# Four chained layers on one core: layer 0's early loads in one queue, the bias table split in compact form and reversed by ScalarE, and batch-norm scales spread from rows

## The chip, the cores and the metric

The kernel runs on one core of one Trainium2 chip. The core has five engines with instruction streams of their own: TensorE (PE, with its weight loads PEld), VectorE (DVE), ScalarE (ACT), GpSimd (POOL) and SyncE (SP). SP, ACT and POOL issue DMAs, which 16 DMA engines carry out. The metric is the device time of one execution in microseconds; the kernel before took 2920.96 us (median of three executions, 2919.23 to 2924.84).

## The reference

The input `x` has the shape (T, B, N, D) = (4, 8, 512, 512), float32. Four layers follow each other, each of the form x + f(groupnorm(x)), with groups of two of the 8 channels (B):

```python
x = x + _L0_conv_ref(_gn(x), ...)   # spiking attention
x = x + _L1_conv_ref(_gn(x), w)     # 13x13 Gaussian, per channel
x = x + _L2_conv_ref(_gn(x), ...)   # 3x3, quantised, 8 channels
x = x + _L3_conv_ref(_gn(x), ...)   # 3x3, 8 channels
```

The change is in layer 0, cut to what matters here (`lif` is a leaky spiking neuron stepping through T; H = 8 heads of 64):

```python
def bn(x, g, b, m, v):
    return g * (x - m) * jax.lax.rsqrt(v + EPS) + b
q = heads(lif(bn(x @ Wq.T, ...)))          # k and v likewise
scores = jnp.einsum('tbhnd,tbhmd->tbhnm', q, k) * scale
rel = pos[None, :] - pos[:, None] + (N - 1)
bias = bias_table[rel].transpose(2, 0, 1)   # table: (1023, 8)
out = jnp.einsum('tbhnm,tbhmd->tbhnd', scores + bias[None, None], v)
out = lif(out) * gate_scale + gate_shift
out = lif(bn(out @ Wp.T, ...))
```

Scores have no softmax, so q (k v) is computed instead of (q k) v. The bias is a Toeplitz matrix for each head: element (n, m) is the table's entry m - n + 511.

## The kernel before

**Order of the work.** The program is written in Python; a scheduler fixes the order of the instructions on each engine when the program is built, and each engine then runs its list strictly in order, waiting on semaphores for others. `tc.issue_after(op)` puts the instructions of a block behind `op` in the lists of engines. Of DMAs that SP and ACT issue, eight are under way at most: each uses one of eight semaphores, and the next on the same one waits for it. Tiles come from pools; tiles with one tag share its buffers, and a new tile waits until the last use of the one before it in that buffer.

**Layer 0** goes through 32 steps (b, t), one image of 512 x 512 each. A step needs the group statistics (mean, deviation) of channel pair g = b // 2 at time t, so two images per group and t; the one that is worked on comes as `xq` (`load_quarters`, four DMAs with rows of 512 B), the other only for its statistics as `xs` (`load_x`, four tiles). The statistics of step 0 are eight `bn_stats` (L431) and a chain of small instructions between VectorE, TensorE (`gps`, L181) and GpSimd (L178 to L198). `transpose` (L618, L480) normalises the image and transposes it in four pieces `xn`. `project_in` (L499) multiplies by the weights `w_v`, `w_k` and `w_q` (the latter two halves of one tile `w_kq`), in four column blocks c of four matmuls each; each 128x512 float32 matmul leaves two records in the trace. VectorE turns each block into spikes. `attend` then multiplies: `ps_kv` (L515), `ps_a` (L527, q times kv) and `ps_b` (L535, the bias times v); `fire` makes the spikes `so`, and `project_out` (L562) multiplies these by `wp` and adds the residual. The next step's projections are interleaved with `project_out` of the present one.

**Preparations in the first step.**

- `batch_norms` turns the 72 columns of `cols` into a scale and an offset for each feature: `a_half`, `c_half`. For q these are used as columns. For v, k and p the scale is multiplied into the weights (L349) and the offset is a tile `c_twice`, so both are wanted along the free dimension, the same in all partitions. `along_free` (L330 to L340) makes that: VectorE scales the identity by one column (`diag`, L336), TensorE multiplies it by ones (L337), four times for 512 features.
- `load_weights`: `w_v` goes out on SP ahead of `xs`; `w_k` and `w_q` go out on ACT's queue behind ScalarE's instruction that writes `c_v` (L350).
- `prepare_bias` (L353 to L369): a Toeplitz row block of a head needs, in partition p, the table's entries from p on, reversed. So each of 8 heads is loaded as a Hankel matrix of 128 x 896 float32 (`hankel`, each partition's row one entry further), and split in three bfloat16 parts `toep` that add up to the float32 value. ScalarE copies the reversed rows to the first part (L365), VectorE subtracts (L366), ScalarE copies the rest (L367), GpSimd subtracts (L368), ScalarE copies again (L369). Two heads are under way at once.
- `prepare_out` loads W_p (1 MB) on ACT's queue, makes p's offset with 16 small matmuls (`shift`, L382), and splits the scaled W_p in two parts `wp` on VectorE and ScalarE (L401 to L407).
- `bands1` builds layer 1's band matrices. Its scratch tile `bands` has the tag `h_p`, which the bias table's second tile `rest` has too. It clears the taps' rows on VectorE (L729), loads the taps (L731), and TensorE's `ps_band` (L741) waits for these; it stands in TensorE's list ahead of the larger part of step 0's attention.

**Layers 1 to 3** are not touched. Layer 1 reads layer 0's result from DRAM through band matmuls (L815), layers 2 and 3 run together (L1118, L1221).

The functions that the diff touches, with the line numbers of the profile:

Of the kernel before, what the change touches and what calls it, by code (L numbers as in the profile page):

```python
# [129 lines left out]
def network(ctx: ExitStack, tc: tile.TileContext, i: dict, out: bass.AP):  # L130
# [30 lines left out]
    nc.vector.tensor_scalar_mul(avg_same, same, 1.0 / n_half)  # L161
# [65 lines left out]
    with ExitStack() as s:  # L227
        head = layer0(
            s, tc, i, x_in, x1d, ident, block, avg, group_stats, st1, norm1, band1d, r1, w_sum, shared
        )  # L230

# [35 lines left out]
def layer0(  # L267
# [43 lines left out]
    ones = wpool.tile([P, P], F32, name="ones")  # L311
    nc.vector.memset(ones, 1.0)

    def batch_norms():

        neg_half = wpool.tile([P, 4, NC], F32, name="nh0")
        nc.vector.memset(neg_half, -0.5)
        nc.vector.tensor_scalar_add(a_half, bn[:, :, 3, :], EPS)
        nc.gpsimd.tensor_tensor(a_half, a_half, neg_half, op=ALU.pow)
        nc.vector.tensor_mul(a_half, a_half, bn[:, :, 0, :])  # L320
        nc.vector.tensor_scalar_mul(a_half, a_half, 0.5)
        c = c_half[:, :3, :]
# [3 lines left out]
        nc.vector.scalar_tensor_tensor(  # L326
            c, bn[:, :3, 1, :], 0.5, c, op0=ALU.mult, op1=ALU.add
        )
# [16 lines left out]
    def prepare_in(n):  # L345
        j = "qkvp".index(n)
        scale = along_free(a_half[:, j, :])
        for k in range(NC):
            nc.vector.tensor_mul(wT[n][:, k, :], wT[n][:, k, :], scale)  # L349
        return nc.scalar.mul(c_twice[n], along_free(c_half[:, j, :]), 2.0).ins  # L350

    def prepare_bias():


        n_u = toep[0].shape[2]
        table = i["table"]
        hankel = state.tile([P, 2, n_u], F32, tag="h_o", name="hankel")
        rest = state.tile([P, 2, n_u], F32, tag="h_p", name="rest")
        for h in range(H):
            src, r = hankel[:, h % 2, :], rest[:, h % 2, :]  # L360
            nc.scalar.dma_start(
                src, bass.AP(table.tensor, h * (2 * N - 1), [[1, P], [1, n_u]])
            )
            dst = [w[:, h, :] for w in toep]
            nc.scalar.copy(dst[0], src[:, ::-1])  # L365
# [3 lines left out]
            nc.scalar.copy(dst[2], r)  # L369
# [6 lines left out]
    def prepare_out(wp32):  # L376
# [3 lines left out]
        for e in range(NC):  # L380
# [11 lines left out]
        nc.vector.scalar_tensor_tensor(c, bn[:, 3, 1, :], 0.5, c, op0=ALU.mult, op1=ALU.add)  # L392

        nc.scalar.mul(
            c_twice["p"].rearrange("p (g v) -> p g v", g=PH), phases(along_free(c)), 2.0
        )
        scale = work.tile([P, D], F32, tag="v", name="scale_p", bufs=3)
        nc.scalar.copy(scale, along_free(a_half[:, 3, :]))
# [256 lines left out]
    for n in range(-1, last + 1):  # L655
# [39 lines left out]
        if n < 0:  # L695
            with ExitStack() as behind:
                for op in first:
                    behind.enter_context(tc.issue_after(op))
                prepare_bias()
# [620 lines left out]
```

## Time and profile before

| what | us |
|---|---|
| median of three executions | 2920.96 (2919.23 to 2924.84) |
| profiled execution: own time | 2921.53 |
| profiled execution: span, first to last instruction | 2919.3 |
| TensorE busy in the span | 2819.7 (97%) |
| VectorE busy | 2208.5 (76%) |
| GpSimd busy | 888.1 (30%) |
| ScalarE busy | 551.0 (19%) |
| DMA, mean over the span | 110 GB/s, 322.10 MB |

The span leaves out what lies before the first and after the last instruction, 2.2 us here. In timelines each line has the start and the duration in us, the engine (ACTq and SPq are issues of DMAs), the line of the code, the operation, the tiles written and read, and in brackets how long the engine had been idle and what ended that wait. Lines of the same kind that follow each other are merged: "x8" and the time of all of them. The granted clock is the share of full speed that TensorE's clock was given in a stretch.

### The profile page before, as it was taken

To read this page: it belongs to the slowest core of one execution; us is meant where nothing else is said; L and a number is where in the kernel's file an instruction comes from. 1 tells how busy PE (TensorE), PEld (TensorE's weight loads), DVE (VectorE), ACT (ScalarE), POOL (GpSimd) and SP (SyncE) were. 2 spreads that over 40 slices of the span, in tenths; PEclk is the share of its full clock that TensorE was granted. 3 is DMA by queue.
4 is the path that set the end of the run, shared out by engine and by line. 5 is a ranking of instruction groups with operands and counts; after the bars stand their busy time and mean duration, and the time that the engine had idled before them with its cause. 6 is when DMAs were issued, how large, how long until landed. Compare 5 with 4: busy or idle time off the path is not lost. (4 is left out here: it accounts for less than half of the span.)

```text
span 2919.3 us, 36593 instructions
## 1 busy us (share of the span) xinstructions
PE 2819.7 (97%) x12865; PEld 1301.8 (45%) x12865; DVE 2208.5 (76%) x3916; ACT 551.0 (19%) x860; POOL 888.1 (30%) x1928
## 2 busy tenths in 40 slices
PE   6899999999999999999999999999999999679999
PEld 3454455554555554455455555545333333223334
DVE  7898688688779868877886886796665566888870
ACT  1300010010010001001000100110111121677774
POOL 3243233334224333323432343332311111232220
PEclk9899999999999999999999999999999999999999
DMA  7332322222322222222222111112877778699975
GB/s 180 96 81 78 79 62 63 70 70 77 73 59 66 69 75 74 69 59 67 69 70 59 45 52 52 52 52 62 226 202 207 201 212 220 170 199 238 219 193 147
DMA packets 323895, 322.10 MB, mean 110 GB/s; under 512 B 21431, under 2 KB 237183, under 8 KB 323599
## 3 DMA queue, kind: packets, MB, share of 16 engines
q1 hardware_dynamic: 261872, 237.39, 33.4%
q0 software_dynamic: 19776, 56.14, 6.0%
q10 hardware_dynamic: 42063, 26.23, 3.2%
q8 instruction: 101, 1.65, 0.3%
q14 instruction: 83, 0.68, 0.1%
HBM read 210.57 MB, written 103.60 MB: 108 GB/s over the span
## 5 line engine op out<-in xcount | busy, mean ns | idle before, releaser
L499 PE MATMUL ps_in<-w_v,xn 128*128 128x512 f32 x1024 | 459.5, 599 | 3.0 <-DVE xn L480 3.0
L499 PE MATMUL ps_in<-w_kq,xn 128*128 128x512 f32 x1024 | 450.1, 592 | 0.0
L815 PE MATMUL ps_conv<-x,bt 112*64 112x512 f32 x2048 | 445.2, 592 | 0.8 <-DVE v_p L467 0.8
L499 PE MATMUL ps_in<-xn,w_kq 128*128 128x512 f32 x1024 | 444.6, 592 | 0.0
L535 PE MATMUL ps_b<-toep,vtok 128*64 128x512 bf16 x3072 | 368.2, 383 | 1.0 <-DVE v_o L550 1.0
L450 ACT ACTIVATE h_q<-v_q,c_half 128x512 f32<-128x512 f32 x96 | 69.2, 721 | 1473.1 <-DVE v_q L446 852.3
L475 POOL TENSOR_TENSOR h_v<-h_v,c_v 128x512 f32<-128x512 f32 x96 | 121.9, 1270 | 686.0 <-DVE h_v L474 660.0
L584 POOL COPY x1s<-x1s 128x2 f32<-128x2 f32 (+1 forms) x1024 | 227.7, 277 | 273.3 <-DVE x1s L573 273.3
L562 PE MATMUL ps_out<-wp,so 128*128 128x512 f32 x1024 | 308.9, 444 | 0.0
L499 PEld LDWEIGHTS ps_in<-xn,w_kq 128*128 128x128 f32 x1024 | 194.3, 190 | 233.0 <-issue 222.0
L499 PEld LDWEIGHTS ps_in<-w_kq,xn 128*128 128x128 f32 x1024 | 194.2, 190 | 219.9 <-issue 205.0
L499 PEld LDWEIGHTS ps_in<-w_v,xn 128*128 128x128 f32 x1024 | 191.0, 191 | 218.5 <-issue 210.2
L815 PEld LDWEIGHTS ps_conv<-x,bt 112*64 112x64 f32 x2048 | 146.4, 135 | 288.9 <-issue 286.5
L535 PEld LDWEIGHTS <-vtok 128*64 128x64 bf16 x3072 | 175.6, 111 | 154.7 <-issue 5.6
L1221 PE MATMUL ps_conv<-x,band_t 64*64 64x512 f32 x2040 | 242.6, 595 | 0.0
L562 PEld LDWEIGHTS ps_out<-wp,so 128*128 128x128 f32 x1024 | 192.6, 188 | 94.4 <-issue 57.8
L1125 DVE SCALAR_TENSOR_TENSOR x<-ps_conv,inv,x 128x512 f32<-128x512 f32 (+1 forms) x172 | 187.4, 1185 | 45.7 <-PE ps_conv L1118 45.6
L573 DVE SCALAR_TENSOR_TENSOR x1s<-v_p,xr 128x256 f32<-128x256 f32 x256 | 188.5, 776 | 14.9 <-DMA x<-x1s 4.1
L837 POOL DMA_DIRECT2D x<-xo x128 | 71.6, 566 | 330.8 <-ACT xo L822 316.4
L822 ACT ACTIVATE xo<-ps_conv,off 128x512 f32<-128x512 f32 x128 | 87.8, 688 | 431.1 <-PE ps_conv L815 310.2
L475 POOL TENSOR_TENSOR h_k<-h_k,c_k 128x512 f32<-128x512 f32 x96 | 123.2, 1284 | 134.0 <-DVE h_k L474 134.0
L1118 PE MATMUL ps_conv<-xq,band 128*128 128x512 bf16 (+1 forms) x516 | 132.2, 393 | 30.3 <-POOL xq L1101 30.3
(193 smaller groups left out, 3161.4 us busy)
## 6 DMA issues: line engine op xcount, KB each, us to landing
x<-x SPq DMA_DIRECT2D x64, 917.0 KB
x<-x SPq DMA_DIRECT2D x168, 256.0 KB
x<-x1s POOLq DMA_DIRECT2D x128, 262.0 KB, 2.6
xq<-in_x SPq DMA_DIRECT2D x128, 256.0 KB
xr<-in_x SPq DMA_DIRECT2D x128, 256.0 KB
out<-o SPq DMA_DIRECT2D x164, 192.0 KB
xs<-in_x SPq DMA_DIRECT2D x112, 256.0 KB
x<-xo ACTq DMA_DIRECT2D x128, 128.0 KB
```

The costliest lines, as they stand in the source:

```text
L475: nc.gpsimd.tensor_add(h, h, c_twice[n])
L499: mm = nc.tensor.matmul(ps, lhsT=lhsT, rhs=rhs, start=k == 0, stop=k == NC - 1)
L535: nc.tensor.matmul(pb[two * DH : (two + 1) * DH, :], lhsT=v[:, c, h * DH : (h + 1) * DH], rhs=toep[z][:, h, u : u + N], start=c == 0 and z ...
L562: nc.tensor.matmul(ps, lhsT=so[:, k, c * P : (c + 1) * P], rhs=wpT[z][:, k, :], start=k == 0 and z == 0, stop=k == NC - 1 and z == 1,)
L573: nc.vector.scalar_tensor_tensor(own, v.rearrange("p (g v) -> p g v", g=PH)[:, two, :], 1.0, by_phase[:, two, :], op0=ALU.is_ge, op1=ALU.add,)
L584: nc.gpsimd.tensor_copy(x1[:, f, u : u + n], x1[:, fm, um - n + 1 : um + 1][:, ::-1])
L815: mm = nc.tensor.matmul(ps[q * M1 : (q + 1) * M1, :], lhsT=bt[:, z, :], rhs=xt[:, w0 : w0 + N_PS1, z : z + NV], start=z == 0, stop=z == SH ...
L822: nc.scalar.activation(xo[:, a, :], ps, AF.Identity, bias=off[:, t : t + 1])
L837: engine.dma_start(bass.AP(dst.tensor, dst.offset + (q * n_half * W1_OUT * B + b) * D + f * NV, [[B * D, W1_OUT], [W1_OUT * B * D, n_half] ...
L1118: mm = nc.tensor.matmul(ps[:n_p, :], lhsT=w["band2"][:n_p, j, dx, :n_p], rhs=xq[:, j, dx : dx + PH, :], start=dx == 0, stop=dx == 2,)
L1125: done["DVE"] = nc.vector.scalar_tensor_tensor(own.rearrange("p (v g) -> p g v", g=PH), by_phase(ps[:n_p, :]), w["inv"][:n_p], by_phase(x[ ...
L1221: mm = nc.tensor.matmul(ps[j][b * HALF : (b + 1) * HALF, :], lhsT=band[half, b, dx, :], rhs=x3[half, s0 + j, dx : dx + D], start=dx == 0, ...
```

## The change

It has four parts.

1. **Loads.** Step 0's `xq`, then `xs`, then the weights of v, k and q all go out on SP in this order. The weights of k and q no longer wait for `c_v`. The batch norms are built first, and the loads' consumers come behind them in VectorE's list. `avg_same`, which waits for the constants' DMA, is now written behind layer 0 in the code.
2. **Scales from rows.** `as_rows_of` transposes all scale columns at once (16 rows of 128) and all offsets at once (12 rows), and copies them from PSUM to SBUF on ScalarE. `along_free` then needs four matmuls whose stationary operand is one column of the identity, broadcast over 128 columns: it picks one row and spreads it over the partitions. The `diag` products on VectorE and the tile `ones` go. For p, the scale comes before the offset now.
3. **The bias table's split.** The table (8 x 1023) is loaded once as 24 x 341, split in its three bfloat16 parts there (five VectorE instructions on 24 partitions), and the parts are written to DRAM as 3 x 8184.
4. **The bias table's turn.** For each pair of heads and each part, a Hankel tile of 128 x 2 x 896 bfloat16 is loaded from these, and one ScalarE copy writes it reversed to `toep`. That is 12 loads and 12 copies. The tile takes the buffer `h_o` if h + z is odd (z = 1) and `h_p` if it is even (z = 0 and z = 2).

In the built program, VectorE's scalings of `w_v` stand behind step 0's transposes, ScalarE's first Hankel loads stand behind its copy of `c_k`, and the statistics sums (`gps`) of steps 1 and 2 come later in TensorE's list than before. W_p's load stands between the first two Hankel loads and the third.

```diff
-    nc.vector.tensor_scalar_mul(avg_same, same, 1.0 / n_half)
...
+    nc.vector.tensor_scalar_mul(avg_same, same, 1.0 / n_half)
...
-    ones = wpool.tile([P, P], F32, name="ones")
-    nc.vector.memset(ones, 1.0)
...
-    def along_free(cols):
+    def as_rows_of(cols):
+
+        n = cols.shape[1]
+        ps = ps_mm.tile([n, P], F32, tag="mm", name="ps_rows")
+        nc.tensor.transpose(ps, cols, ident)
+        rows = wpool.tile([4 * NC, P], F32, tag="rows", name="rows", bufs=2)
+        nc.scalar.copy(rows[:n], ps)
+        return rows[:n]
+
+    def along_free(rows, j):
 
 
+        n = rows.shape[0]
         ps = ps_mm.tile([P, D], F32, tag="mm", name="ps_free")
         for c in range(NC):
-            diag = work.tile([P, P], F32, tag="diag", name="diag", bufs=2)
-            nc.vector.tensor_scalar_mul(diag, ident, cols[:, c : c + 1])
+            at = NC * j + c
             nc.tensor.matmul(
-                ps[:, c * P : (c + 1) * P], lhsT=ones, rhs=diag, start=True, stop=True
+                ps[:, c * P : (c + 1) * P], lhsT=ident[:n, at : at + 1].to_broadcast([n, P]),
+                rhs=rows, start=True, stop=True,
             )
         return ps
...
     def prepare_in(n):
         j = "qkvp".index(n)
-        scale = along_free(a_half[:, j, :])
+        scale = along_free(a_rows, j)
         for k in range(NC):
             nc.vector.tensor_mul(wT[n][:, k, :], wT[n][:, k, :], scale)
-        return nc.scalar.mul(c_twice[n], along_free(c_half[:, j, :]), 2.0).ins
-
-    def prepare_bias():
-
-
-        n_u = toep[0].shape[2]
-        table = i["table"]
-        hankel = state.tile([P, 2, n_u], F32, tag="h_o", name="hankel")
-        rest = state.tile([P, 2, n_u], F32, tag="h_p", name="rest")
-        for h in range(H):
-            src, r = hankel[:, h % 2, :], rest[:, h % 2, :]
-            nc.scalar.dma_start(
-                src, bass.AP(table.tensor, h * (2 * N - 1), [[1, P], [1, n_u]])
-            )
-            dst = [w[:, h, :] for w in toep]
-            nc.scalar.copy(dst[0], src[:, ::-1])
-            nc.vector.tensor_sub(r, src[:, ::-1], dst[0])
-            nc.scalar.copy(dst[1], r)
-            nc.gpsimd.tensor_sub(r, r, dst[1])
-            nc.scalar.copy(dst[2], r)
+        return nc.scalar.mul(c_twice[n], along_free(c_rows, j), 2.0).ins
+
+    n_h, n_u = 2 * N - 1, toep[0].shape[2]
+
+    def split_bias():
+
+        n_e = n_h // 3
+        parts = tc.dram_tile([3, H * n_h], BF16, name="bias_parts")
+        src = state.tile([3 * H, n_e], F32, tag="h_o", name="bias_table")
+        nc.scalar.dma_start(src, bass.AP(i["table"].tensor, 0, [[n_e, 3 * H], [1, n_e]]))
+        part = state.tile([3 * H, 3, n_e], BF16, tag="h_p", name="bias_part")
+        for z in range(3):
+            nc.vector.tensor_copy(part[:, z, :], src)
+            if z < 2:
+                nc.vector.tensor_sub(src, src, part[:, z, :])
+        nc.scalar.dma_start(
+            bass.AP(parts.tensor, parts.offset, [[n_e, 3 * H], [H * n_h, 3], [1, n_e]]), part
+        )
+        return parts
+
+    def prepare_bias(parts):
+
+
+        for h in range(0, H, 2):
+            for z in range(3):
+                hankel = state.tile(
+                    [P, 2, n_u], BF16, tag="h_o" if (h + z) % 2 else "h_p", name="hankel"
+                )
+                nc.scalar.dma_start(
+                    hankel,
+                    bass.AP(
+                        parts.tensor, parts.offset + (z * H + h) * n_h, [[1, P], [n_h, 2], [1, n_u]]
+                    ),
+                )
+                nc.scalar.copy(toep[z][:, h : h + 2, :], hankel[:, :, ::-1])
...
-    load(0)
-    load_weights("v", nc.sync)
-    statistics(0, 0, 0, as_rows(xs[0]))
-    statistics(0, 0, 1, load_x(1, 0, "xs"))
-    batch_norms()
+    normed = batch_norms()
+    a_rows = as_rows_of(a_half.rearrange("p n c -> p (n c)"))
+    c_rows = as_rows_of(c_half[:, :3, :].rearrange("p n c -> p (n c)"))
+    with tc.issue_after(normed):
+        load(0)
+        statistics(0, 0, 0, as_rows(xs[0]))
+        statistics(0, 0, 1, load_x(1, 0, "xs"))
+        for n in "vkq":
+            load_weights(n, nc.sync)
+        bias_parts = split_bias()
     for k in range(NC):
         transpose(0, k)
-    with tc.issue_after(prepare_in("v")):
-        load_weights("k", nc.scalar)
-        load_weights("q", nc.scalar)
+    prepare_in("v")
```

Left out of the diff: in `prepare_out`, p's scale is spread and copied ahead of p's offset (which goes through `as_rows_of`), and the call of `prepare_bias` passes the parts.

More of the change, by code (lines that the diff above doesn't have):

```diff
@@ L325, in batch_norms @@
         )
[L326 removed]
+        op = nc.vector.scalar_tensor_tensor(
             c, bn[:, :3, 1, :], 0.5, c, op0=ALU.mult, op1=ALU.add
         )
[L330 removed]
+        return op.ins
+    def as_rows_of(cols):
[7 more added lines that the diff above has]
+        n = rows.shape[0]
         ps = ps_mm.tile([P, D], F32, tag="mm", name="ps_free")
         for c in range(NC):
[L335 to L336 removed]
+            at = NC * j + c
             nc.tensor.matmul(
[L338 removed]
+                ps[:, c * P : (c + 1) * P], lhsT=ident[:n, at : at + 1].to_broadcast([n, P]),
+                rhs=rows, start=True, stop=True,
             )
@@ L392, in prepare_out @@
         nc.vector.scalar_tensor_tensor(c, bn[:, 3, 1, :], 0.5, c, op0=ALU.mult, op1=ALU.add)
+        scale = work.tile([P, D], F32, tag="v", name="scale_p", bufs=3)
+        nc.scalar.copy(scale, along_free(a_rows, 3))
         nc.scalar.mul(
-            c_twice["p"].rearrange("p (g v) -> p g v", g=PH), phases(along_free(c)), 2.0
+            c_twice["p"].rearrange("p (g v) -> p g v", g=PH), phases(along_free(as_rows_of(c), 0)), 2.0
         )
-        scale = work.tile([P, D], F32, tag="v", name="scale_p", bufs=3)
-        nc.scalar.copy(scale, along_free(a_half[:, 3, :]))
         for k in range(NC):
@@ L698, in layer0 @@
                     behind.enter_context(tc.issue_after(op))
-                prepare_bias()
+                prepare_bias(bias_parts)
                 prepare_out(load_out())
```

## The prediction

> **What bounds the kernel now.** First the page's busy shares and slices:
>
> ```profile
> PE 2819.7 (97%) x12865; PEld 1301.8 (45%) x12865; DVE 2208.5 (76%) x3916; ACT 551.0 (19%) x860; POOL 888.1 (30%) x1928
> PE   6899999999999999999999999999999999679999
> ```
>
> TensorE is busy 97% of the span. The holes are the first two slices (146 us) and one near 2,500 us, where layer 1 gives way to layer 2. The diff touches layer 0's start only, and of the built programs' orders of instructions TensorE's agree again some 380 instructions in, the others' within the first two steps. A gain in the first slices moves everything behind it forward, since TensorE idles only 1.9 us between 200 and 250 us. So I read the head in stretches of 20 us (busy time of each engine, TensorE's granted clock, DMA share, GB/s):
>
> ```profile
> 0.00:20.00 20.00, 4.74 (x16) 3.71 (x16) 8.35 (x28) 1.88 (x2) 4.42 (x8) 1.00 0.97 191
> 20.00:40.00 20.00, 8.97 (x24) 5.09 (x25) 11.41 (x26) 0.00 (x0) 1.92 (x2) 1.00 0.89 213
> 80.00:100.00 20.00, 16.68 (x104) 9.92 (x104) 17.18 (x27) 10.59 (x13) 7.16 (x4) 0.74 0.63 144
> 100.00:120.00 20.00, 9.60 (x44) 5.13 (x45) 14.79 (x32) 7.87 (x13) 0.38 (x1) 0.58 0.41 116
> 120.00:140.00 20.00, 20.00 (x77) 9.29 (x74) 16.77 (x34) 3.06 (x5) 7.35 (x14) 1.00 0.09 29
> ```
>
> There are two holes: before about 40 us, with the DMA engines full, and 80 to 120 us, with TensorE often idle and at a low clock. From 120 us it is full. The timeline tells what ends the first:
>
> ```profile
> 22.43 1.36 DVE L431 BATCH_NORM_STATS2 st<-xs 128x6 f32<-128x512 f32 x2 [5.26 <-DMA xs<-in_x]
> 25.48 0.17 DVE L178 TENSOR_REDUCE gsum_x<-st 128x1 f32<-128x16 f32 x1
> 30.96 5.60 PE L499 MATMUL ps_in<-w_v,xn 128*128 128x512 f32 x8 [3.00 <-DVE xn L480]
> ```
>
> The first projection starts at 30.96, 5.5 us after the last statistics, which waited for `xs`. In the second hole TensorE's own timeline reads:
>
> ```profile
> 79.44 3.93 PE L382 MATMUL shift<-cols,wp 128*128 128x1 f32 x32
> 107.90 1.91 PE L741 MATMUL ps_band<-bands 13*52 13x128 f32 x8 [6.76 <-DMA bands<-in_w]
> 112.50 0.56 PE L181 MATMUL gps_x<-gsum_x,avg 128*128 128x1 f32 x2 [2.68 <-DVE gsum_x L178]
> 131.76 2.43 PE L562 MATMUL ps_out<-wp,so 128*128 128x512 f32 x8
> ```
>
> Its three projections end at 79.4; `ps_band` waits until 107.9; the first output projection, my mark for "the head is over", comes at 131.8. `bands` lies in the buffer `h_p`, which the bias table frees last:
>
> ```profile
> 69.24 0.33 ACTq L361 DMA_DIRECT2D hankel<-in_table  x1
> 70.66 2.10 DVE L504 TENSOR_SCALAR k<-v_k 128x512 bf16<-128x512 f32 x1
> 72.51 0.94 ACT L369 CAST toep<-rest 128x896 bf16<-128x896 f32 x1 [2.40 <-DMA hankel<-in_table]
> 86.32 0.34 ACTq L361 DMA_DIRECT2D hankel<-in_table  x1
> 94.11 0.94 ACT L365 CAST toep<-hankel 128x896 bf16<-128x896 f32 x1 [1.31 <-DMA hankel<-in_table]
> 101.17 0.94 ACT L369 CAST toep<-rest 128x896 bf16<-128x896 f32 x1
> ```
>
> The last piece is copied at 102.1; from there to `ps_band` are 5.8 us (memset, the taps' DMA). A head's rows took 3.3 us from issue (69.24) to use (72.51) with nothing else moving, 7.8 us (86.32 to 94.11) beside the loads of step 2.
>
> **What the Trainium skill says.** "DMA: Bandwidth & Descriptors", section "Issuing engines are not separate DMA queues": DMAs of all issuers run on the same 16 engines and interleave. The trace agrees: `xs` went out with w_k and w_q from the other queue at a DMA share of about 1.05, and came late. "ScalarE: Activation LUTs", section "What ACT_TABLE_LOAD costs": with immediate operands 186 ns plus 0.833 ns an element, fp32 and bf16 alike. That gives 932 ns for 896 elements; the trace has 936, reversed reads included, and 618 for 512. "GPSIMD Engine Reference", section "1. Specifications": its SBUF interfaces are shared with VectorE. The trace agrees: the threshold above took 2.10 us while GpSimd subtracted (70.19 to 72.48), about 0.4 otherwise. "TensorE: Matmul & The Clock Gate", part 1: half clock after an idle window, until it has been busy about 3.4 us; the trace shows 0.50 granted from 104 to 120 us.
>
> **The change, part by part.**
>
> *Loads in order.* Ahead of the first normalisation must land xq and xs (1.05 MB each), c128 (0.18), cols and the table (0.07): 2.35 MB. In the trace 2.1 MB had moved by 12 us at some 215 GB/s, so `xs` is complete at 13, not 24. One statistics instruction (0.7) and the 5.5 us chain make 19.2; but the scalings of w_v, formerly done while waiting, now stand behind the transposes: three further transposes (1.85) and the first scaling (0.67) give 21.7 for the first projection, 9.2 earlier. w_v lands by 18.1 (another 1.05 MB), w_k by 23, w_q by 28, ahead of need at about 21, 35 and 51. Ahead of it all VectorE gets five passes over 24x341 elements (2 us by 128x512 rows of 0.4 to 0.7) that wait for the table's 33 KB: cols, first in that queue, landed at 3.85, xq needs 7, so they cost nothing. If the table came 10 us late, the statistics behind it would be as late.
>
> *Scales from rows.* VectorE loses 24 `diag` instructions of 0.28 us, and TensorE its waits for them. The first four matmuls (5.4, from 30.96) end at 27.1; eight small ones at 0.3 end at 29.5; 44 matmuls at 0.87 (two records of 0.434: 32 in 13.90) end at 67.8, some 68 with two statistics sums. Before: 79.4. That is 11.4 earlier.
>
> *Bias table.* Off the engines go 8 VectorE subtractions (1.08), 8 GpSimd ones (1.9) with the stretching they cause, and 24 ScalarE copies (22.5 us); 12 ScalarE copies of 1792 elements come (estimate by the skill's price 1.68; 20.2 us), and 12 loads of 459 KB in rows of 1792 B for 8 in rows of 3584 B. There are two buffers, and z = 0 and z = 2 share one, so eight loads and copies go one after the other through `h_p`; the order pairs the first four with one in `h_o`. The first goes out behind the c_k copy, at 29.5. For a load I take 3.7 alone (3.3 plus 0.4 for shorter rows, a guess), 5.5 beside others, 1.7 for a pair's second. Round 1, beside xq and xs of step 1: 29.5 + 5.5 + 1.7 + 1.7 = 38.4. Round 2 stands behind the 1.05 MB of w_p: 1.97 MB at half of 300 GB/s end at about 43, lands 46 and 47.7, copied 49.4. Rounds 3 and 4: 7.1 each, 63.6. Two singles at 5.5: 74.6; two beside step 2's loads at 7.3: 89.2. Plus the same 5.8: `ps_band` at 95, 12.9 earlier. Bounds of a load: 3.3 and 7.8 us, both measured. ScalarE's h_q copies and w_p casts stand between the later copies, with VectorE's results behind them; those inputs come at 57 to 80 us, and I count nothing.
>
> *After `ps_band`.* Before: 23.9 us to the mark. The 2.7 us wait for a statistics sum goes (it now stands behind the projection), about 1 us of waits for v_o too: 20.2, hence 115.2. That is 16.6 earlier; I take 16. Moving `avg_same` is nothing: its reader is in layer 2.
>
> Against the profiled execution (2921.53 around a span of 2919.3; 0.6 above the median 2920.96) this gives 2905.5, against the median **2905.0**.
>
> **Rivals.**
>
> *The bias chain is hidden.* With 3.3 us for every load and no delay by w_p the chain is 29.5 + 4 x 6.7 + 4 x 5.0 = 76, `ps_band` 82, the mark 102; TensorE's own work from 68 (w_p sums 3.9, attention 14, eight matmuls 7, small ones 2) allows 95. That is 2891 at 102, 2884 at the floor. Against it: w_p and step 1's loads are in the same engines.
>
> *The serial chain becomes the bound (slower).* If each load takes the loaded 7.8 us, four paired rounds of 11.2, w_p's 5 and four singles of 9.5 end at 117, `ps_band` at 123, the mark at 143: 11 later, 2932. For it: one buffer for eight transfers, 5.5 MB instead of 3.7, half the row length. Against it: from 64 to 70 us the DMA engines were empty. It decides from a chain end of about 106, 2 us more on each of eight rounds.
>
> *Only the start is gained, or nothing.* If the chain ends near 100, the mark is at 126: 2915. If it also stalls w_p's casts, nothing is left: 2921. A bf16 copy at twice the estimated price would do it (20 us).
>
> **How the numbers follow.** What a measurement of this kernel tells from no change is about 0.2%, 5.8 us. Main case (2898 to 2912) 0.55; hidden chain 0.15; start only, 2912 to 2915, 0.11; within 0.2% 0.10; slower 0.09. Faster is 0.81. Leaving out about one in ten below and above gives 2890 to 2922.
>
> **What would show it.** First projection near 21.7 us, projections done near 68, last bias copy near 89, `ps_band` near 95, the mark near 115; TensorE idle from about 78 to 95, and GpSimd without subtractions. An early first projection with a mark beyond 126 means the load chain was mis-sized; a first projection at 28 or later, that the single queue is slower than 215 GB/s or the table's load held VectorE. A shift at the mark unlike that of the end would refute that TensorE carries it on.

## The result and the profile after

The changed kernel takes 2902.18 us (median of four executions, 2901.55 to 2903.70) against 2920.60 for the kernel before in the same measurement (2919.23 to 2924.84). The ratio is 0.9936, 95% interval 0.9924 to 0.9948: faster by 0.64%, or 18.4 us. The profiled execution took 2902.63 us around a span of 2900.8, against 2921.53 and 2919.3 before: the span is 18.5 us shorter, and what lies around it is the same to 0.4 us.

Line numbers shift with the diff: the projections are now L524, `ps_band` L769, the mark's `ps_out` L587, the reversing copies L394 and the Hankel loads L388.

First the page's busy shares and TensorE's slices:

```profile
PE 2818.8 (97%) x12868; PEld 1302.5 (45%) x12868; DVE 2183.1 (75%) x3888; ACT 549.2 (19%) x851; POOL 868.8 (30%) x1920
PE   7999999999999999999999999999999999689999
```

TensorE has the same work as before (2818.8 against 2819.7 us). VectorE has 25 us less and GpSimd 19 us less, and neither difference is the gain: the gain is idle time of TensorE, by far the most of it in the first two slices (some 2 us lie between 1150 and 1480 us, see the last part on the prediction). The stretches show it (length, busy time of PE, PEld, DVE, ACT and POOL, granted clock, DMA share, GB/s):

```profile
0.00:20.00 20.00, 5.64 (x22) 4.66 (x22) 11.16 (x32) 2.39 (x4) 4.95 (x9) 1.00 0.85 192
20.00:40.00 20.00, 17.34 (x46) 8.43 (x47) 11.84 (x21) 3.97 (x3) 2.53 (x2) 1.00 0.78 184
80.00:100.00 20.00, 13.69 (x90) 7.40 (x88) 11.86 (x23) 8.53 (x15) 0.00 (x0) 0.70 0.64 154
100.00:120.00 20.00, 19.75 (x83) 9.61 (x79) 19.33 (x43) 3.05 (x6) 5.73 (x13) 1.00 0.48 125
120.00:140.00 20.00, 19.70 (x56) 10.18 (x55) 19.11 (x34) 0.00 (x0) 13.67 (x26) 1.00 0.22 77
```

From 20 to 40 us TensorE is busy for 17.3 us where it was 9.0, and from 100 to 120 us for 19.75 where it was 9.6. The second hole is down to one stretch, 80 to 100 us. GpSimd's subtractions are gone there (7.16 us of work before, none now).

The timeline, TensorE's but for the first line:

```profile
14.83 0.17 DVE L177 TENSOR_REDUCE gsum_x<-st 128x1 f32<-128x16 f32 x1
22.66 5.94 PE L524 MATMUL ps_in<-w_v,xn 128*128 128x512 f32 x8 [5.35 <-DVE w_v L359]
...
70.80 6.30 PE L407 MATMUL shift<-cols,wp 128*128 128x1 f32 x32
89.68 0.64 PE L552 MATMUL ps_a<-q,kvb 128*64 128x512 f16 x2 [2.33 <-DVE kvb L545]
93.87 1.91 PE L769 MATMUL ps_band<-bands 13*52 13x128 f32 x8 [3.56 <-DMA bands<-in_w]
111.25 2.11 PE L587 MATMUL ps_out<-wp,so 128*128 128x512 f32 x8
...
222.48 0.64 PE L552 MATMUL ps_a<-q,kvb 128*64 128x512 f16 x2 [2.89 <-DVE kvb L545]
```

The statistics are summed at 14.83 instead of 25.48, the first projection starts at 22.66 instead of 30.96, `ps_band` at 93.87 instead of 107.90, the mark comes at 111.25 instead of 131.76. Between the projections' end (68.9) and 87.3 us TensorE has no gap. It is slow there, though: the 16 one-column matmuls of `shift` (32 records) take 6.30 us where they took 3.93, and in finer stretches the granted clock is 0.50 from 71.6 to 81.8 us.

ScalarE's timeline has the bias table's loads (ACTq) and copies:

```profile
30.68 0.92 ACTq L388 DMA_DIRECT2D hankel<-bias_parts  x2
...
46.37 3.27 ACT L394 COPY toep<-hankel 128x1792 bf16<-128x1792 bf16 x2 [7.74 <-DMA hankel<-bias_parts]
...
77.73 1.69 ACT L394 COPY toep<-hankel 128x1792 bf16<-128x1792 bf16 x1 [2.06 <-DMA hankel<-bias_parts]
79.45 0.37 ACTq L388 DMA_DIRECT2D hankel<-bias_parts  x1
...
85.88 0.25 ACT L336 COPY rows<-ps_rows 4x128 f32<-4x128 f32 x1 [5.34 <-PE ps_rows L334]
...
87.09 1.68 ACT L394 COPY toep<-hankel 128x1792 bf16<-128x1792 bf16 x1
```

The bias chain, from the issue of the first load to the end of the last copy, runs from 30.68 to 88.77, which is 58.1 us; before, it was 57.6 (44.49 to 102.11). It is no shorter, it starts earlier. In this execution its last link is not a load: ScalarE stood for 5.34 us at the copy of the rows of p's offset, which waits for TensorE, and the last bias copy is behind that in ScalarE's list.

### The profile page after: what moved, and what is told of

Read it like the earlier page. It is cut to its first block, busy times and chain, and to the rows that moved or that the text cites. A ratio compares the mean times of both kernels' runs of the same rounds, so it can differ in the third digit from the quotient of the medians.

```text
span 2900.8 us, 36559 instructions
## 1 busy us (share of the span) xinstructions
PE 2818.8 (97%) x12868; PEld 1302.5 (45%) x12868; DVE 2183.1 (75%) x3888; ACT 549.2 (19%) x851; POOL 868.8 (30%) x1920
## 5 line engine op out<-in xcount | busy, mean ns | idle before, releaser
L524 PE MATMUL ps_in<-w_v,xn 128*128 128x512 f32 x1024 | 459.1, 599 | 5.4 <-DVE w_v L359 5.4
L524 PE MATMUL ps_in<-w_kq,xn 128*128 128x512 f32 x1024 | 449.8, 592 | 0.0
L524 PE MATMUL ps_in<-xn,w_kq 128*128 128x512 f32 x1024 | 444.9, 592 | 0.0
L587 PE MATMUL ps_out<-wp,so 128*128 128x512 f32 x1024 | 308.7, 444 | 0.0
L524 PEld LDWEIGHTS ps_in<-xn,w_kq 128*128 128x128 f32 x1024 | 194.3, 190 | 232.5 <-issue 220.4
L524 PEld LDWEIGHTS ps_in<-w_kq,xn 128*128 128x128 f32 x1024 | 194.3, 190 | 220.7 <-issue 206.2
L524 PEld LDWEIGHTS ps_in<-w_v,xn 128*128 128x128 f32 x1024 | 191.4, 191 | 222.9 <-issue 212.1
L587 PEld LDWEIGHTS ps_out<-wp,so 128*128 128x128 f32 x1024 | 192.6, 188 | 94.0 <-issue 57.8
```

The lines of the kernel that those rows point to most:

```text
L524: mm = nc.tensor.matmul(ps, lhsT=lhsT, rhs=rhs, start=k == 0, stop=k == NC - 1)
L587: nc.tensor.matmul(ps, lhsT=so[:, k, c * P : (c + 1) * P], rhs=wpT[z][:, k, :], start=k == 0 and z == 0, stop=k == NC - 1 and z == 1,)
```

## The experiments

All kernels compute the whole result. "Median" is the time of a kernel; the ratio is that to the kernel before, run on the same chip.

### What each of three parts carries

Each kernel is the changed one with one part put back.

**The old making of the bias table**, with the new loads and rows kept:

```diff
-        bias_parts = split_bias()
...
-                prepare_bias(bias_parts)
+                prepare_bias()
```

Here `prepare_bias` is the old one: 8 float32 Hankel loads, 24 copies, subtractions on VectorE and GpSimd.

> The changed kernel with the bias table made the old way (8 float32 Hankel loads, three ScalarE copies, one VectorE and one GpSimd subtraction a head); loads and scales stay changed. Theory A, the bias rework carries part of the gain (it frees VectorE and GpSimd and shortens the chain): last bias copy after 92 us, ps_band after 97, time 2906 to 2912. Theory B, the gain comes from the earlier start alone, since the chain from the first Hankel load to the last copy was 57.6 us before (44.5 to 102.1) and is 58.1 now (30.7 to 88.8): the old chain, started some 14 us earlier, ends by 88, first projection at 20.5 because the split is gone from the front of VectorE's list, time 2898 to 2903.

Measured: 2911.22 (2910.08 to 2913.58), ratio 0.9971 (0.9959 to 0.9983). The first projection starts at 22.14, 0.5 us earlier without the split on 24 partitions. The last bias copy ends near 92.8, `ps_band` comes at 101.92, the mark at 121.33. The chain is 63.1 us long here (29.70 to 92.77), 5 more than in the changed kernel. Part of what is lost is no bias chain at all. A line of TensorE's timeline of this kernel, and two that lie side by side on GpSimd and VectorE:

```profile
73.46 0.59 PE L180 MATMUL gps_x<-gsum_x,avg 128*128 128x1 f32 x2 [7.56 <-DVE gsum_x L177]
...
42.66 2.06 POOL L378 TENSOR_TENSOR rest<-rest,toep 128x896 f32<-128x896 f32 x1
42.90 2.37 DVE L484 SCALAR_TENSOR_TENSOR h_v<-v_v 128x512 f32<-128x512 f32 x1
```

VectorE is busy for 18.5 of the 20 us from 40 to 60 us, against 10.7 in the changed kernel, and so is late with the next step's statistics. Only 3.3 us of that are its own subtractions. Four other instructions of that stretch take 2.1 to 2.4 us instead of 0.4 to 0.7, each of them while GpSimd subtracts. So the old subtractions cost VectorE more through GpSimd than by its own share.

**The old order of loads:**

```diff
+    load(0)
+    load_weights("v", nc.sync)
+    statistics(0, 0, 0, as_rows(xs[0]))
+    statistics(0, 0, 1, load_x(1, 0, "xs"))
+    batch_norms()
...
-        for n in "vkq":
-            load_weights(n, nc.sync)
...
+    with tc.issue_after(prepare_in("v")):
+        load_weights("k", nc.scalar)
+        load_weights("q", nc.scalar)
```

> The changed kernel with the loads as before: w_v on SP ahead of xs, w_k and w_q on ACT's queue behind c_v, statistics ahead of the batch norms in the code. Theory A and B: first projection at 30 to 32 us, the first Hankel load at 38 to 40, everything behind it 8 us later, time 2909 to 2912. Rival, the start is covered by later waits (the wait for ps_band and the cold clock): first projection as late, but the mark (first output projection) within 4 us of 111, time 2903 to 2906.

Measured: 2910.11 (2909.42 to 2910.60), ratio 0.9966 (0.9953 to 0.9979). The first projection starts at 33.04, the first Hankel load is issued at 40.32, the last bias copy ends at 95.7, `ps_band` comes at 99.76 and the mark at 119.38. A start that is 10.4 us later makes the end 7.9 us later. The start is also later than was expected, and 2.1 us later than in the kernel before: VectorE's wait for `xs` ends at 25.17 here, at 22.43 there. So this variant costs a little more than the old order did in its own kernel.

**The old `diag` products** in place of the rows:

```diff
-            at = NC * j + c
+            diag = work.tile([P, P], F32, tag="diag", name="diag", bufs=2)
+            nc.vector.tensor_scalar_mul(diag, ident, cols[:, c : c + 1])
             nc.tensor.matmul(
-                ps[:, c * P : (c + 1) * P], lhsT=ident[:n, at : at + 1].to_broadcast([n, P]),
-                rhs=rows, start=True, stop=True,
+                ps[:, c * P : (c + 1) * P], lhsT=ones, rhs=diag, start=True, stop=True
             )
```

> The changed kernel with scales and offsets spread by the old diag products (24 VectorE instructions) instead of rows. If the rows pay, as the prediction had it (TensorE's waits for diag between the first blocks, 2.2 us of the 11.4 by the end of the projections): first projection within 1 us of 22.7, projections done at 70.5 to 73, time 2904 to 2907. Rival, VectorE has room at that time (busy 54% from 40 to 60 us) and hides them: within 1 us of 2902.

Measured: 2910.32 (2907.65 to 2911.56), ratio 0.9963 (0.9949 to 0.9977): a miss, by some 3 us to the slow side. First projection 25.57 (expected within 1 us of 22.7), projections done at 72.4, first Hankel load 36.28, `ps_band` 99.06, mark 117.88. From VectorE's and ScalarE's timelines:

```profile
12.86 2.46 DVE L449 BATCH_NORM_STATS2 st<-xq 128x6 f32<-128x512 f32 x4
36.21 0.60 ACT L353 ACTIVATE c_k<-ps_free 128x512 f32<-128x512 f32 x1 [22.96 <-PE ps_free L340]
```

The rows do more than take work from VectorE: without them ScalarE's copy of `c_k` comes 5.6 us later (36.21 instead of 30.61), and the whole bias chain hangs on that copy. Of these, 2.9 us are there at the start: the first `diag` products stand ahead of the statistics in VectorE's list, which begin at 12.86 instead of 9.94. In the kernel before they cost nothing there, as the last statistics waited for `xs` until 22.43. And only 4.3 of the 8.1 us arise in the head: step 3's first `ps_kv` starts at 287.80 instead of 283.47. The rest comes between 1150 and 1480 us, as is told in the part on the prediction.

Putting one part back costs 9.0, 7.9 and 8.1 us; that is 25.0 for three parts of a change that gains 18.4. The costs are not to be added up: each of the parts delays the start of the same bias chain, or lengthens it, and the variants have costs that the kernel before did not have (the start of the old loads, `diag` ahead of the statistics).

### Is the length of the bias chain what sets the end?

**Longer: all Hankel tiles in one buffer.**

```diff
-                    [P, 2, n_u], BF16, tag="h_o" if (h + z) % 2 else "h_p", name="hankel"
+                    [P, 2, n_u], BF16, tag="h_p", name="hankel"
```

> The changed kernel with all twelve Hankel tiles in the buffer h_p, so loads and copies go strictly one after the other: the rival mechanism of the prediction, made worse on purpose. If the end of the chain decides, as I hold: 12 rounds of about 5.9 us (4.2 load, 1.7 copy) and some 4 for w_p from 30.7 give a last copy near 105, ps_band near 111, the mark near 127, time 2916 to 2921. Rival, TensorE is held by something else (the copy of c_p's rows and the product kvb, not the table): ps_band within 5 us of 93.9, time within 5 us of 2902.

Measured: 2915.83 (2912.67 to 2918.62), ratio 0.9984 (0.9978 to 0.9991); the time is just below what was expected, and so is the mark; the last copy (105.4) is where it was expected. TensorE's timeline:

```profile
97.52 0.64 PE L552 MATMUL ps_a<-q,kvb 128*64 128x512 f16 x2 [8.09 <-ACT v_o L570]
...
105.43 2.35 PE L560 MATMUL ps_b<-toep,vtok 128*64 128x512 bf16 x20 [1.30 <-ACT toep L394]
108.81 1.04 PE L769 MATMUL ps_band<-bands 13*52 13x128 f32 x8 [1.02 <-DMA bands<-in_w]
```

Now TensorE waits longest for `v_o` (8.09 us), which stands behind a bias copy in ScalarE's list, and then for `toep` itself (1.30). A chain end 16.6 us later makes the mark 12.7 us later (123.97) and the end 13.7 by the medians (11.4 between the profiled executions): a longer chain costs most of its length.

**Shorter: strict alternation of the two buffers**, so that two loads in a row never use the same one. It was run twice on one chip, the second time together with the changed kernel:

```diff
-                    [P, 2, n_u], BF16, tag="h_o" if (h + z) % 2 else "h_p", name="hankel"
+                    [P, 2, n_u], BF16, tag="h_o" if (3 * h // 2 + z) % 2 else "h_p", name="hankel"
```

> The changed kernel with the twelve Hankel tiles in strict alternation over h_o and h_p, so that one loads while the other is copied. If the end of the chain alone decides: last bias copy near 77 us instead of 88.8, ps_band near 83, the mark (first output projection) near 100, time 2891 to 2895. If, with the chain out of the way, ps_band falls to the next thing in line (the taps' load stands behind W_p's casts in ACT's list, and these behind the copy of c_p's rows, which waits for TensorE): last copy near 77, but ps_band at 91 to 95, time within 4 of 2902.

> Strict alternation of the buffers once more: 2900 within 1.5 us, and 1 to 3 us below the changed kernel on the same chip.

> The changed kernel once more, with nothing edited, on the same chip as the two others: 2902 within 1.5 us; the mark at 111.3 within 0.5 us. If it lies more than 2 us from 2902.2, differences of 2 us between kernels are not told apart by runs on different chips.

Measured: alternation 2900.09 (2899.07 to 2901.33), ratio 0.9931 (0.9916 to 0.9946), the second time 2903.89 (2902.03 to 2904.97), ratio 0.9942 (0.9930 to 0.9955); the changed kernel again 2903.58 (2902.09 to 2905.36), ratio 0.9942 (0.9929 to 0.9954). The last copy ends at 77.5 and 79.4, 11 and 9 us earlier than in the changed kernel's profile above (9 and 7 earlier than in its second one, where it ends at 86.2), and the time is the same. What looked like 2 us in the first measurement did not come back in the second. The alternation's own two measurements differ by 3.8 us, on one chip, so differences of up to 4 us between measurements are not read from here on.

Where the 9 us go is seen in the second run of the alternation, in VectorE's timeline and one line of TensorE's:

```profile
79.94 1.16 DVE L426 SCALAR_TENSOR_TENSOR wp_k<-wp,cols,scale_p 128x512 f32<-128x512 f32 x1 [5.37 <-ACT scale_p L419]
...
88.79 0.61 DVE L545 TENSOR_TENSOR kvb<-ps_kv,c 128x512 f16<-128x512 f32 x1
89.46 0.64 PE L552 MATMUL ps_a<-q,kvb 128*64 128x512 f16 x2 [5.23 <-DVE kvb L545]
```

ScalarE's copy of `scale_p` stands behind the last two bias copies. VectorE waits 5.37 us for it, then does the whole preparation of W_p, and `kvb` is behind that in its list. The TensorE wait that was for the bands in the kernel before (6.76 us) is now for the larger part one for `kvb` (5.23; 2.75 for the bands are left), and VectorE starts `kvb` no earlier than in the changed kernel (88.79 against 88.94, and 86.13 in that kernel's second profile).

**The rows of p's offset copied by VectorE**, so that ScalarE does not stand in front of the last bias copy:

```diff
-    def as_rows_of(cols):
+    def as_rows_of(cols, copy=nc.scalar.copy):
...
-        nc.scalar.copy(rows[:n], ps)
+        copy(rows[:n], ps)
...
-            c_twice["p"].rearrange("p (g v) -> p g v", g=PH), phases(along_free(as_rows_of(c), 0)), 2.0
+            c_twice["p"].rearrange("p (g v) -> p g v", g=PH), phases(along_free(as_rows_of(c, nc.vector.tensor_copy), 0)), 2.0
```

> The changed kernel with one copy moved: c_p's rows go from PSUM to SBUF on VectorE instead of ScalarE, so that ScalarE's last bias copy no longer stands behind a copy that waits 5.3 us for TensorE. If this head-of-line wait held the end of the chain: last bias copy ends at 84 to 86 instead of 88.8, ps_band 89 to 92, time 2898 to 2901. If the load (issued at 79.5) was what came last: copy at 88.8 and time as before, 2902.

Measured: 2904.05 (2903.18 to 2905.09), ratio 0.9944 (0.9927 to 0.9961): no gain. ScalarE now waits at the next instruction of its list:

```profile
85.62 0.62 ACT L432 CAST wp<-wp_k 128x512 fp32r<-128x512 f32 x1 [4.14 <-DVE wp_k L431]
```

That cast waits for VectorE, which waits for TensorE's `ps_rows` (84.40). The last bias copy ends at 87.8 instead of 88.8. So in these two executions its time is set by when TensorE comes to `ps_rows`. In the changed kernel's second profile TensorE comes there at 82.26, ScalarE waits 1.12 us for it, and the last copy starts at 84.55, 4.2 us after the issue of its load (80.34). There the load may have been as late as the list, which the trace does not tell apart.

### An earlier start, another buffer for the bands

**The bands' scratch in `h_o`**, the buffer that comes free first:

```diff
-    scratch = state.tile([P, 2 * P + B * n_w + PH * n_p + B], F32, tag="h_p", name="bands1")
+    scratch = state.tile([P, 2 * P + B * n_w + PH * n_p + B], F32, tag="h_o", name="bands1")
```

> The changed kernel with the scratch of layer 1's bands in the buffer h_o, free at about 62 us, instead of h_p: the taps are loaded long before ps_band, the bias chain is as before. If ps_band was held by its buffer, as I read it: ps_band at 87 to 89, straight behind the product before it, TensorE's 3.6 us wait gone, what remains is set by kvb and the last bias copy at 88.8; mark 106 to 108, time 2897 to 2900. Rival: TensorE waits as long for the last bias copy or for v_o instead, time within 2 of 2902.

Measured: 2907.92 (2905.90 to 2913.56), ratio 0.9960 (0.9946 to 0.9975), slower than the changed kernel by 4.3 to 5.7 us (its two measurements), which neither side had expected. VectorE's timeline:

```profile
64.62 0.18 DVE L757 MEMSET bands<- 13x152 f32 x1 [4.66 <-ACT toep L394]
```

The clearing of `bands` moves up in VectorE's list, comes there before ScalarE's copy has freed the buffer, and holds up everything behind it for 4.66 us. The next step's statistics come late, and TensorE then waits 3.71 us for their sum at 70.94.

**The scalings of `w_v` between the transposes**, each as soon as its piece is transposed, with the table's split behind the last of them; once with the bands in `h_o`, once with the alternation and the bands left in `h_p`:

```diff
+    def piece(k):
+        with tc.issue_after(scaled["v"]) if k else ExitStack():
+            transpose(0, k)
+        return transposes[-1]
+
+    prepare_in("v", piece)
+    with tc.issue_after(scaled["v"]):
         bias_parts = split_bias()
-    for k in range(NC):
-        transpose(0, k)
-    prepare_in("v")
```

> A candidate: bands in h_o as above, the scalings of w_v in turn with step 0's transposes instead of behind them, and the table's split behind both in VectorE's list. If the start carries through: first projection at 20.0 to 20.8 us instead of 22.7, everything behind 2 us earlier than with bands in h_o alone, time 2894 to 2898. If w_v lands too late for this (its last piece was issued at 16.3 us): first projection at 22 or later and the time of bands in h_o alone.

> Both edits that helped: the loads alternate strictly between h_o and h_p, the scalings of w_v stand between the transposes, and the table's split stands behind the first scaling; the bands' scratch stays in h_p. Theory 'no single bound, two chains within a few us of each other': the first projection at about 20.5, the last bias copy at about 77 to 79, `ps_band` near 89, the mark at about 107 to 109, the time 2897 to 2900. Rival 'the start is absorbed by the next in line' (TensorE's own small matmuls and VectorE's statistics around 65 to 90): the mark at 108.7 as with the alternation alone, time within 1.5 us of it (2900.1).

Measured: with the bands in `h_o` 2905.87 (2904.44 to 2908.12), ratio 0.9951 (0.9936 to 0.9966); with the alternation 2903.22 (2901.16 to 2903.41), ratio 0.9937 (0.9924 to 0.9951), on the same chip as the 2903.58 above. The first projection does start earlier, at 20.52 and 20.81. In the second kernel the last bias copy ends at 75.9, too, 13 us before the changed kernel's; the mark is at 111.93 all the same. A start 1.9 us earlier and a chain that ends 13 us earlier are worth nothing together. TensorE waits 5.00 us for `kvb` (at 90.95) in this kernel, too.

### The preparation of W_p behind `kvb`

The alternation's kernel, with `prepare_out` written into the first step's attention, behind `kvb` and the first head pair:

```diff
+            if meanwhile and j == 0:
+                with tc.issue_after(masked):
+                    meanwhile()
...
-                so = attend(spikes, t)
+                so = attend(spikes, t, (lambda: prepare_out(wp32)) if n == 0 else None)
...
-                prepare_out(load_out())
+                wp32 = load_out()
```

> Strict alternation of the buffers as before, and `prepare_out` is written into the first step's attention, behind the instruction that makes `kvb`: VectorE's W_p scalings and subtractions, ScalarE's `scale_p` copy and W_p casts come behind `kvb`, the clearing of `bands` and the first `v_o`, and some of the next step's projections come ahead of the last heads' products in TensorE's list. Theory 'W_p's preparation, which ScalarE does behind the last bias copies and VectorE ahead of `kvb`, is what TensorE waits for once the bias chain is shorter': no wait of 5 us for `kvb`, `ps_a` at 81 to 83, `ps_band` at about 85 to 87, TensorE's idle time between 80 and 120 us down from 9.8 (alternation, second time) to about 4, the time 2896 to 2899. Rival 'the preparation of 9 us is serial wherever it stands': the wait comes back at `v_o` or at `ps_b`, idle time and time as before, 2902 to 2904.

Measured: 2907.74 (2906.57 to 2909.23), ratio 0.9958 (0.9944 to 0.9971), no gain, and 7.7 and 3.9 us above the alternation's two measurements, the smaller of which is the edge of what is read here. Neither side had that. TensorE's timeline:

```profile
77.66 0.41 PE L552 MATMUL ps_a<-q,kvb 128*64 128x512 f16 x2 [1.99 <-DVE kvb L545]
...
107.04 0.69 PE L590 MATMUL ps_out<-wp,so 128*128 128x512 f32 x2 [3.09 <-DVE so L469]
...
163.44 0.64 PE L552 MATMUL ps_a<-q,kvb 128*64 128x512 f16 x2 [6.80 <-DVE kvb L545]
```

The local steps went as the first theory said, and better: `kvb` at 77, `ps_band` at 84.91, and TensorE busy for 19.6 of the 20 us from 80 to 100. The time did not fall. With W_p's inputs later in TensorE's list, VectorE had nothing to do but for 5.6 us of that stretch (11.9 in the changed kernel), did W_p from 92 to 108 us, and was full from there on (19.3 of 20 us from 100 to 120, 39.7 of 40 from 120 to 160). TensorE then waited for it: at `so`, and 6.80 us for the next step's `kvb`. The rival had the direction (the wait comes back elsewhere) and was 4 us too low. In this kernel, then, the work that VectorE has not done by 100 us is made up for in steps 0 and 1, and TensorE waits for it there. One thing besides the order differs: the clock is 0.50 from 78 to 95 us, and `shift` takes 6.98 us. Whether this variant would gain without that is not known.

## Why the prediction was right

It forecast 2905.0 with a main range of 2898 to 2912; 2902.18 was measured. The main case held, and most of its steps did, by their own times (us from the span's start). In the changed kernel's second profile the last copy ended at 86.2, `ps_band` came at 91.57 and the mark at 109.52; where forecast and measurement agree to less than 2 us from there on, some of it is luck.

| step | predicted | measured |
|---|---|---|
| first projection | 21.7 | 22.66 |
| projections done | 68 | 68.9 |
| first Hankel load issued | 29.5 | 30.68 |
| round 1 copied | 38.4 | 38.6 |
| round 2 copied | 49.4 | 49.6 |
| rounds 3 and 4 copied | 63.6 | 63.6 |
| two singles copied | 74.6 | 74.0 |
| third single | 81.9 | 79.4 |
| last copy | 89.2 | 88.8 |
| `ps_band` | 95 | 93.87 |
| mark | 115.2 | 111.25 |
| earlier at the mark | 16.6 | 20.5 |
| earlier at the end | 16 | 18.5 |

**Loads in order: right.** `xs` was in by the time the statistics asked for it; their last instruction ended at 14.8, where the working gave 13.7, and the first projection is as much later. The path was another one than in the working: not the last piece of `xs` sets this end, but the eight statistics one after the other, 4.9 us without a pause, from 9.94 on. What they wait for at the start is `xq`, which the working had at 7: in the three kernels without the split ahead of them VectorE waited for `xq` until 9.43, 9.59 and 9.88. The split, counted as nothing, thus delays them by 0.5 us at most.

**Scales from rows: right in its sum, too small as a thing of its own.** The working credited it with `diag` instructions and waits among the projections. That the chain's first load comes 5.6 us earlier through it was only in the total; putting `diag` back costs 8 us, nearly half of them far behind the head.

**Bias table: right, with the last two terms wrong in opposite directions.** Up to the second single the loads came within 0.6 us of the sum, in part because errors cancelled: the first load went out 1.2 us late, and round 1 then took 8.0 us instead of 8.9. The price of a load alone, 3.3 us, was read up to the copy at 72.51, but that copy reads `rest` and not the load; the quickest load of the changed kernel took 3.7 us from issue to use (74.00 to 77.73), which is what the prediction had set for one with shorter rows. The copies cost 1.69 us each; the estimate from the Trainium skill, "ScalarE: Activation LUTs", section "What ACT_TABLE_LOAD costs", was 1.68, and this trace bears it out for bfloat16 and 1792 reversed elements. The singles beside step 2's loads were then priced at 7.3 us and the third took 5.4. The sentence "I count nothing" for ScalarE's other work between the copies failed: the last copy stood behind the rows' copy, which waited 5.34 us for TensorE. The one error hid the other, and the sum came out at 88.8 for 89.2; that is luck. That the wait is real and not cured by moving it is shown by the kernel in which VectorE copies the rows.

**TensorE idle from 78 to 95: wrong.** It had no gap until 87.3. Half clock for 10 us is one part of this. In the second profile, with 3.4 us of half clock, TensorE was still busy until 84.0 but for 0.37 us: 15.6 us from the projections' end (68.4), for which the forecast allowed 10 (68 to 78) and shows no working. The gap which was left is 87.3 to 93.9, with 2.33 us of waiting for `kvb` and 3.56 for the bands in it.

**After `ps_band`: a term mis-sized.** 20.2 us were allowed to the mark, 17.4 were needed; that is 2.8 of the 4 us by which the mark was missed, the other 1.1 is `ps_band`. Of the wait for the statistics nothing was left, and 0.41 of 0.96 us of that for `v_o`.

**"A shift at the mark unlike that of the end": this sign came, and TensorE carries the gain on only in part.** The lead over the kernel before is 20.5 us at the mark, 15.9 at step 3, the same until some 1150 us, 18.1 at 1458 and 18.5 at the end. TensorE's lines at the start of `ps_kv`, before and after in turn:

```profile
299.41 1.06 PE L515 MATMUL ps_kv<-vtok,k 128*128 128x128 bf16 x16
283.47 1.06 PE L540 MATMUL ps_kv<-vtok,k 128*128 128x128 bf16 x16
...
1476.16 1.06 PE L515 MATMUL ps_kv<-vtok,k 128*128 128x128 bf16 x16
1458.07 1.06 PE L540 MATMUL ps_kv<-vtok,k 128*128 128x128 bf16 x16
```

So 4.6 us are lost behind the mark. Four waits make 2.2 of them, each for VectorE: 0.25 and 0.30 us for a statistics sum (115.33, 123.61), 0.64 for `kvb` (157.81), and 2.89 instead of 1.86 for `kvb` of step 2 (222.48 in the timeline above). Behind the last one the clock is 0.50 for some 3 us, and the next 16 records of `ps_b` take 3.02 us instead of 1.89. Most of the remainder, about 1 us, are three statistics sums that stood ahead of the mark before. VectorE is busy for 19.1 to 19.3 of each 20 us from 100 to 140 us; before, it had 35.2 us of work in the 40 from 120 to 160.

And 2.2 us come back between 1150 and 1480 us, where all engines have the same order of instructions as before: TensorE waits for `kvb` in three steps for 1.47, 2.13 and 1.24 us in the kernel before, for 0.81, 1.71 and not at all in the changed one. The kernel with `diag` put back waits there as well (1.31, 2.25, 0.99); each of the twelve traces of kernels without `diag` gains 2.0 to 2.9 us there. So this goes with the `diag` products, which are long over by then; why is open.

The forecast took 16 us from the mark to the end. The lead at the mark was 4 us more than forecast, 4.6 were lost behind it where 0.6 were allowed, and 2.6 came later from where nothing was forecast: that the forecast lies within 2.8 us of the result is in part luck.

**The rivals.** The serial chain as the bound did not come about, but it was no empty case: with one buffer for all loads the chain ended at 105.4, next to the 106 from which the prediction said it would decide, and 13.7 of the 18.4 us were gone by the medians. The hidden chain (2891, or 2884 at TensorE's floor) is refuted by the alternation: the chain then ends at 77.5 to 79.4 as that rival wanted, and the mark does not move to 102. Its floor left out VectorE's preparation of W_p, which comes after the chain in that kernel and ahead of `kvb`.

What stays open: which of TensorE's half clock, ScalarE's list and VectorE's W_p work would have to go first for a time below 2900. Each was changed alone or not at all; no kernel without the half clock around `shift` was tried. That the half clock alone is worth much is unlikely: it lasted 10 us in one profile of the changed kernel and 3.4 in the other, and the spans are equal. None of the variants was faster than the changed kernel by more than the 3.8 us by which the alternation's two measurements differ.

## What to carry to other kernels

When a stall has been taken out, look at what stands next in each in-order list before taking out more: here a chain that ended another 9 to 13 us earlier gave nothing, since other work was right behind it in the same lists, while ending it 17 later cost 14. Undo parts one at a time, and do not add up what they cost. Follow a gain past the place where it is made: 20.5 us at the mark were 15.9 by step 3. And when an engine is full in the steady stage behind a head, as VectorE was here, its idle time in the head counts as well as that of the engine that sets the end.

## What the runs showed of the hardware

**TensorE's clock fell to half during the one-column matmuls or right behind them, at a moment that differs from execution to execution.** The same changed kernel in its second profile:

```profile
70.27 3.73 PE L407 MATMUL shift<-cols,wp 128*128 128x1 f32 x32
...
109.52 2.11 PE L587 MATMUL ps_out<-wp,so 128*128 128x512 f32 x8
```

Here `shift` took 3.73 us instead of 6.30. The granted clock was 0.50 from 74.1 to 77.4 us only, instead of 71.6 to 81.8, and the mark came 1.7 us earlier, at an equal span (2900.8 both times). In eleven of the fourteen traces the clock falls during `shift` or less than 2 us behind it, with no gap of over 0.2 us in TensorE's work for 6 us before; in the other three, TensorE had waited for 2.0 to 3.7 us shortly before. The Trainium skill, "TensorE: Matmul & The Clock Gate", part 1, section "What's actually happening", says that the clock is granted by a window which runs freely, so that the moment depends on where in the window the work falls; these two executions agree, with moments 2.5 us apart, more than the 0.5 us either way that the section gives for a kernel's first matmul. It names idle windows as what lowers the clock; in the profile TensorE counts as busy for 20 of the 20 us from 60 to 80, so that the small matmuls seem to count as little or no activity. This is inferred from where the clock fell; no kernel with these matmuls left out or made wider was run.

**A mark within the kernel can vary by more than the end.** Two executions of the changed kernel differ by 1.7 us at the mark and by nothing at the end, and two of the alternation by 2.8 us at the mark (108.67 and 111.49) and 2.5 in the span. By these four profiles, a step of less than about 3 us should not be read from one of them.
